# A feed-forward pair's transposes moved between the next pair's second and third quarter

## The chip, the cores and the metric

The kernel runs on one core of one Trainium2 chip. The metric is the device time of one execution in microseconds; three runs of the kernel before gave 3746.26 us as their median (3743.07 to 3754.74). A profile is one further execution recorded by the hardware profiler. The engines are named as the profile names them: PE (TensorE, matmul), PEld (its weight loads), DVE (VectorE), ACT (ScalarE), POOL (GpSimd) and SP (SyncE, which here only issues DMAs).

## The reference

Two layers on x of shape (4, 512, 128, 64): four batch entries, 512 times, 128 frequencies of 64 channels, D = 8192 values at each time, all in float32.

Layer 0, for each batch entry:

```python
xn = layernorm(x)                                  # over D
k, v, r = xn @ Wk, xn @ Wv, sigmoid(xn @ Wr)       # 64 states
s = scan(decay * s + k * v)                        # over time
x = x + (r * s) @ Wo                               # attention
x = x + gelu(conv over the 128 frequencies of layernorm(x))
to = layernorm(depthwise causal conv over time, 3 taps, of layernorm(x))
x = x + to
x = x + (gelu(x @ ffn_W1 + ffn_b1) @ ffn_W2 + ffn_b2)   # 64 -> 256 -> 64
```

Layer 1 takes a moving average over 25 times as the trend, transforms the rest over time with a real FFT, mixes 128 modes with complex weights, transforms back and adds the trend. The change touches only the last line of layer 0, the feed-forward, and how the stages of other batch entries are woven into it.

## The kernel before

In layer 0 the tensors lie with 128 of the D values on the partitions and the 512 times along the free dimension: 64 chunks of 128 x 512 per batch entry, handled in 32 pairs (NPR). The stages of an entry are generator functions: `project` (J, L324), `scan` (Z, L419), `attend_and_convolve` (A, L514), `convolve_time` (C, L645), `open_feed` (O, L705) and `feed_forward` (F, L713). Each `yield` hands over a weight, the share of the stage that has been put out.

`in_turn` (L822) weaves two lines of stages. Its list names for each step which stage of which batch entry runs in the one line and which in the other: F of entry 0 beside J and Z of entry 2, F of 1 beside J and Z of 3, F of 2 beside C and O of 3, and at last F of 3 beside nothing. At every yield it looks which of the two lines is behind and lets that one go on to its next yield. On PE the order so written is the order of execution (`manual_schedule`, L860). On the other engines the framework's scheduler orders the instructions, apart from those that are pinned to the program's order with `keep_in_program_order`. All engines wait for each other through semaphores, and a tile's buffer is reused only once its readers are done.

`run` (L812) keeps a set, `narrowly`. It holds the other stage while that is attention or while its last yield was a step of a chain (a scan, or the broadcast of statistics); it is empty beside the plain steps of `project` and `convolve_time`.

The feed-forward treats a pair in four quarters of the 256 hidden channels:

- `widen(i, q)` (L726; its matmul is L731) multiplies pair i with a quarter of W1: four matmuls of 64 x 64 weights into one of two PSUM units, m and c, which `unit` (L722) gives out alternately. ACT then applies the gelu (L736) and writes `mid`, four buffers.
- `narrow(i, q)` (L738; its matmul is L744) multiplies `mid` with a quarter of W2 and adds it up over the four quarters in two PSUM accumulators, p and pb, each with one buffer. After the fourth quarter DVE adds bias and residual (L757, once for p and once for pb) and writes the pair's result to x4t (three buffers) or, in the last two batch entries, to a wx tile (two buffers).
- `store(i)` (L759) brings the result to time-major form: eight 128 x 128 transposes on PE (L763) into a unit, copies on ACT to `ob` (L771 or L776), and for every second pair a DMA from POOL's queue to x4 (L772). It therefore takes one turn of the same two units that widen uses.

Widen runs two quarters ahead of narrow: in quarters 0 and 1 pair i's own third and fourth widen come, in quarters 2 and 3 the next pair's first two. In quarter 1 the loads and first steps of the residual for pair i + 2 are put out (`residual`, L685: SP's DMAs kx and kh at L605, DVE L690 and L691), in quarter 3 its end (`add_residual`, L694: ACT L699, pinned, and DVE L702).

The loop of the kernel before does this for pair i: first `store(i - lag)`, then the four quarters, then for the first two batch entries one piece of `convolve_ahead` (L633: the first 14 pairs of the next entry's time convolution, in alternate pieces DVE L612 and L615, and ACT L620 with DVE L624), then the yield. Where `narrowly` isn't empty it yields after every quarter. The lag is 1 for entries 0 and 1, and 2 for entries 2 and 3.

So the order on PE around a pair's border, beside a plain stage, is: narrow of the last quarter, the other line's matmuls (L408 for `project`, L251 for `convolve_time`), the transposes, a widen, the next pair's first narrow.

Also touched: `scale_weights` (L354; its instruction L357, DVE) multiplies projection weights by the layernorm's gain. For entries 2 and 3 the call for all steps but the first is pinned. The statistics of these entries (L340) are pinned too.

Of the kernel before, what the change touches and what calls it, by code (L numbers as in the profile page):

```python
# [24 lines left out]
NPR = NCH // 2  # L25
# [54 lines left out]
def layer0(ctx, tc, dram, x, xt, vecs, wkvr, wo, wdec, wconv, fbias, w1, fb1, w2, fb2, x4):  # L80
# [5 lines left out]
    B = x.shape[0]  # L86
# [17 lines left out]
    def two(pool, tag):  # L104
        return pool.tile([P, 2, SL], F32, tag=tag, name=tag)
# [214 lines left out]
    narrowly = set()  # L320
# [3 lines left out]
    def project(b):  # L324
# [36 lines left out]
        ws, xps, xks = {}, {}, {}  # L361
        if b > 1:
            weights(0)
            scale_weights(0, ws[0])
            xps[0] = load_x(b, 0)
        for i in range(NPR):
            first, last = i == 0, i == NPR - 1
# [345 lines left out]
    def feed_forward(b):  # L713
        x3s = opened.pop(b)
        mids, x4s, obs, sums2 = {}, {}, {}, {}
        lag = 1 if b + 2 < B else 2
        turn = [0]
        while not free_s[0]:
            yield BLOCKED
        feeding[0] = True  # L720

        def unit():  # L722
            turn[0] ^= 1
            return two(ps_m, "m") if turn[0] else c_bank()

        def widen(i, q):  # L726
            x3 = x3s[i]
            pm = unit()
            for h in range(2):
                for j in range(2):  # L730
                    nc.tensor.matmul(  # L731
                        pm[halves[j], h, :], lhsT=w1_sb[halves[h], q * H : (q + 1) * H], rhs=x3[halves[h], j, :],
                        start=True, stop=True,
                    )
            mid = mids[i, q] = bk.tile([P, 2, SL], F32, tag="mid", name="mid", bufs=4)
            nc.scalar.activation(mid, pm, AF.Gelu_apprx_tanh, bias=fb1_sb[:, q : q + 1])  # L736

        def narrow(i, q):  # L738
            if q == 0:
                sums2[i] = of_p(), ps_s.tile([P, SL], F32, tag="s", name="pb")  # L740
            mid = mids.pop((i, q))
            for h in range(2):
                for j in range(2):
                    nc.tensor.matmul(  # L744
                        sums2[i][j][halves[h], :], lhsT=w2_sb[halves[j], q, :], rhs=mid[halves[j], h, :],
                        start=q == 0, stop=q == 3,
                    )
            if q < 3:
                return
            x3 = x3s.pop(i)  # L750
            if lag > 1:
                pair = spare("wx", 4 * S + SL)[:, :, 0:SL]
                x4s[i] = [pair[:, j, :] for j in range(2)]
            else:
                x4s[i] = [bk.tile([P, SL], F32, tag="x4t", name="x4t", bufs=3) for _ in range(2)]
            for j, pa in enumerate(sums2.pop(i)):
                nc.vector.scalar_tensor_tensor(x4s[i][j], pa, fb2_sb, x3[:, j, :], ALU.add, ALU.add)  # L757

        def store(i):  # L759
            pt = unit()  # L760
            for j, x4t in enumerate(x4s.pop(i)):
                for t in range(NT):
                    nc.tensor.transpose(pt[:, j, t * P : (t + 1) * P], x4t[:, t * P : (t + 1) * P], ident)  # L763
            s = i // 2
            if i % 2 == 0:
                obs[s] = bk.tile([P, NT, SL], F32, tag="ob", name="ob")
            o = obs[s][:, :, i % 2 * 2 * P : (i % 2 + 1) * 2 * P].rearrange("p t (j w) -> p j t w", j=2)
            pt = pt.rearrange("p j (t w) -> p j t w", t=NT)
            if i % 2:
                for h in range(2):  # L770
                    nc.scalar.copy(o[:, :, :, halves[1 - h]], pt[:, :, :, halves[h]])  # L771
                nc.gpsimd.dma_start(  # L772
                    x4[b][:, s * SL : (s + 1) * SL].rearrange("(t p) d -> p t d", p=P), obs.pop(s)
                )
            else:
                nc.scalar.copy(o, pt)  # L776

        early = None
        done = 0.0
        quarter = 2.25 * (NPR + 1) / (NPR + lag)  # L780
        widen(0, 0)
        widen(0, 1)
        for i in range(NPR + lag):
            if i >= lag:
                store(i - lag)
            for q in range(4):
                done += quarter
                if i < NPR:
                    if q < 2:
                        widen(i, q + 2)  # L790
                    elif i + 1 < NPR:
                        widen(i + 1, q - 2)
                    if i + 2 < NPR and q == 1:
                        coming = residual(b, i + 2)
                    if i + 2 < NPR and q == 3:
                        x3s[i + 2] = add_residual(b, i + 2, *coming)
                    narrow(i, q)
                if q == 3 and b + 2 < B and i > 1:
                    early = early or convolve_ahead(b + 1, lambda: unit()[:, 0, :])
                    next(early, None)  # L800
                if q == 3 or narrowly:
                    yield done
                    done = 0.0
        feeding[0] = False


# [380 lines left out]
```

## Time and profile before

| | |
|---|---|
| median of three runs | 3746.26 us |
| the profiled execution | 3747.14 us |
| its span | 3745.2 us |
| mean granted PE clock | 0.974 |
| PE busy | 3536.6 us, 94% |
| DVE busy | 2669.1 us, 71% |
| ACT busy | 1759.4 us, 47% |
| POOL busy | 522.6 us, 14% |
| HBM traffic | 243 GB/s over the span |

The feed-forwards take these stretches of the span: entry 0 from about 831 to 1235 us, entry 1 from 1490 to 1890, entry 2 from 2145 to 2503, entry 3 from 2503 to 2757; layer 1 takes the last 988 us.

How to read the lines below. In a group, the columns are the line of the kernel, engine, operation, output and inputs with their sizes and the count; then busy time and the mean of one instruction in ns; then the engine's idle time just before these instructions, and what ended most of it. In the timeline, a line has start, duration, engine, line, operation, and in brackets the idle time before it and what ended it. In the table by stretch, a line has its window, length, each engine's busy time, the granted PE clock as a share of full speed, the busy share of the DMA engines and GB/s. A float32 matmul of the program shows as two instructions in the trace.

### The profile page before, as it was taken

The numbers are of one execution on the slowest core, as the hardware profiler recorded it, in microseconds if no ns is written. First come the engines' busy times: TensorE is split into PE (matmuls) and PEld (weight loads), VectorE is DVE, ScalarE is ACT, GpSimd is POOL, SyncE is SP. The second block draws the span as 40 slices with busy tenths as digits, with TensorE's granted clock in tenths as the row PEclk, the third lists the DMA queues.
The fourth block names the chain that finished last, engine by engine and source line by source line (L and its number), as shares of the span: only waits on it lengthen the run. The fifth ranks groups of instructions, "written<-read, shape, count | busy, mean of one in ns | idle before, by whom it ended". The sixth has DMA issues, their size and how long they took to land. (4 is left out here: it accounts for less than half of the span.)

```text
span 3745.2 us, 53017 instructions
## 1 busy us (share of the span) xinstructions
PE 3536.6 (94%) x20041; PEld 1368.8 (37%) x20041; DVE 2669.1 (71%) x3498; ACT 1759.4 (47%) x2299; POOL 522.6 (14%) x782
## 2 busy tenths in 40 slices
PE   9999999999998999999999989999988999989998
PEld 4433322234333223433322233333323843328533
DVE  4445569976776896677789799946667277892677
ACT  0013346655656565565656578868854200142100
POOL 0000012310101121001112122100013000130000
PEclk9999999999999999999999999999999999999999
DMA  9867648787875688788568678645567478993687
GB/s 316 276 206 245 226 163 269 255 280 267 288 263 169 233 279 273 267 292 281 178 231 285 214 248 267 232 152 192 201 233 262 156 235 294 316 322 127 214 285 265
DMA packets 429269, 913.42 MB, mean 244 GB/s; under 512 B 33240, under 2 KB 83672, under 8 KB 424920
## 3 DMA queue, kind: packets, MB, share of 16 engines
q1 hardware_dynamic: 351088, 636.91, 52.4%
q0 software_dynamic: 75776, 271.62, 20.0%
q8 instruction: 160, 2.62, 0.3%
q10 hardware_dynamic: 2152, 1.51, 0.1%
q14 instruction: 93, 0.76, 0.1%
HBM read 641.40 MB, written 268.50 MB: 243 GB/s over the span
## 5 line engine op out<-in xcount | busy, mean ns | idle before, releaser
L744 PE MATMUL p<-mid,w_sb 64*64 64x512 f32 x2048 | 554.8, 599 | 20.2 <-DVE wx L757 20.2
L744 PE MATMUL pb<-mid,w_sb 64*64 64x512 f32 x2048 | 536.7, 599 | 0.0
L736 ACT ACTIVATE mid<-c,fb_sb 128x1024 f32<-128x1024 f32 x256 | 284.6, 1112 | 97.5 <-PE c L731 95.1
L736 ACT ACTIVATE mid<-m,fb_sb 128x1024 f32<-128x1024 f32 x256 | 284.9, 1113 | 93.6 <-PE m L731 92.2
L731 PE MATMUL c<-x,w_sb 64*64 64x512 f32 x2016 | 280.7, 610 | 13.2 <-ACT mid L736 6.9
L731 PE MATMUL m<-x,w_sb 64*64 64x512 f32 x2016 | 283.2, 613 | 6.7 <-ACT ob L776 4.9
L744 PEld LDWEIGHTS p<-mid,w_sb 64*64 64x64 f32 x2048 | 155.5, 135 | 294.8 <-issue 261.6
L408 PE MATMUL a<-xp,wx 128*128 128x512 f32 x512 | 241.7, 615 | 9.1 <-DVE wx L357 8.6
L1032 ACT COPY two<-a 128x512 f32<-128x512 f32 x64 | 37.5, 586 | 428.3 <-PE a L1027 428.3
L1055 PE MATMUL b<-xin,avg_sb 128*128 128x512 f32 x512 | 230.8, 593 | 3.3 <-DVE xin L1061 3.3
L1061 DVE TENSOR_TENSOR xin<-b,pm 128x512 f32<-128x512 f32 x256 | 159.1, 684 | 98.0 <-PE b L1058 83.1
L569 ACT ACTIVATE sq<-x 128x1024 f32<-128x1024 f32 x128 | 135.1, 1055 | 179.4 <-DVE x L566 179.2
L624 DVE SCALAR_TENSOR_TENSOR to<-kd,vec,to 128x510 f32<-128x510 f32 (+1 forms) x272 | 197.2, 745 | 9.9 <-ACT to L620 8.7
L924 DVE COPY xf<-b 128x256 f32<-128x256 f32 x128 | 54.4, 425 | 199.1 <-PE b L1001 179.9
L699 ACT ACTIVATE kd<-kd,vec 128x512 f32<-128x512 f32 x256 | 192.8, 803 | 3.2 <-DVE kd L691 3.2
L251 PE MATMUL st<-x,ones 128*32 128x512 f32 x512 | 173.0, 609 | 12.8 <-DVE x L566 12.8
L624 DVE SCALAR_TENSOR_TENSOR z<-x,vec,z 128x511 f32<-128x511 f32 x240 | 175.9, 745 | 5.3 <-ACT z L620 3.0
L702 DVE TENSOR_TENSOR x<-kd,kx 128x1024 f32<-128x1024 f32 x126 | 154.1, 1223 | 32.6 <-ACT kd L699 32.5
L530 DVE TENSOR_TENSOR x<-a,xp 128x1024 f32<-128x1024 f32 x128 | 156.1, 1220 | 29.1 <-PE a L528 26.9
L528 PE MATMUL a<-rst,wo_sb 64*128 64x512 f32 x512 | 149.2, 657 | 25.1 <-DVE x L530 23.3
L567 POOL DMA_DIRECT2D x<-x x128 | 93.6, 731 | 560.4 <-DVE x L566 544.7
L757 DVE SCALAR_TENSOR_TENSOR x4t<-p,fb_sb,x 128x512 f32<-128x512 f32 x64 | 47.9, 748 | 170.6 <-PE pb L744 168.1
(267 smaller groups left out, 6859.6 us busy)
## 6 DMA issues: line engine op xcount, KB each, us to landing
xp<-in_xt SPq DMA_DIRECT2D x256, 512.0 KB
xin<-x SPq DMA_DIRECT2D x128, 1024.0 KB
kh<-to SPq DMA_DIRECT2D x156, 512.0 KB
x<-x POOLq DMA_DIRECT2D x128, 512.0 KB, 4.6
kx<-x SPq DMA_DIRECT2D x128, 512.0 KB
x<-ob POOLq DMA_DIRECT2D x64, 1024.0 KB, 7.9
out<-xin POOLq DMA_DIRECT2D x64, 1024.0 KB, 6.3
x<-x SPq DMA_DIRECT2D x96, 512.0 KB
```

Source lines behind the costliest of these rows:

```text
L251: nc.tensor.matmul(st[32 * q : 32 * q + 32, :], lhsT=ones, rhs=src[:, j, :], start=first, stop=last,)
L408: nc.tensor.matmul(pa[:, k, :], lhsT=wq[:, j, k * P : (k + 1) * P], rhs=xp[:, j, :], start=first and j == 0, stop=last and j == 1,)
L528: nc.tensor.matmul(at[:, j, :], lhsT=wo_sb[js, :], rhs=rst[js, :], start=True, stop=True)
L530: nc.vector.tensor_tensor(x1, at, xp, ALU.add)
L624: tap = nc.vector.scalar_tensor_tensor(to[:, j, k:], xr[:, j, : SL - k], vec[:, w, c], to[:, j, k:], ALU.mult, ALU.add)
L699: tc.keep_in_program_order(nc.scalar.activation(d[:, j, :], d[:, j, :], AF.Identity, bias=vec[:, B4, c], scale=vec[:, G4, c]))
L702: nc.vector.tensor_tensor(x3, d, x2, ALU.add)
L731: nc.tensor.matmul(pm[halves[j], h, :], lhsT=w1_sb[halves[h], q * H : (q + 1) * H], rhs=x3[halves[h], j, :], start=True, stop=True,)
L736: nc.scalar.activation(mid, pm, AF.Gelu_apprx_tanh, bias=fb1_sb[:, q : q + 1])
L744: nc.tensor.matmul(sums2[i][j][halves[h], :], lhsT=w2_sb[halves[j], q, :], rhs=mid[halves[j], h, :], start=q == 0, stop=q == 3,)
L1055: nc.tensor.matmul(po[j], lhsT=avg_sb[:, j, :], rhs=xin[:, j, :], start=True, stop=False)
L1061: nc.vector.tensor_tensor(by_n(xin[:, j, :]), by_n(po[j]), by_c(pm[j % 2][:, j // 2, :]), ALU.add)
```

## The change

The transposes of pair i - lag no longer stand ahead of pair i's first quarter but between its second and third. The regular yield, at which the other line is let in, stands there too, just ahead of the transposes, and not at the pair's end. Where `narrowly` isn't empty, there is still a yield ahead of each of the other quarters. The lag of the last batch entry becomes 1 (its results stay in wx tiles); that of entry 2 stays 2. The pairs past the end, which only store, yield first. The first scaling of projection weights for entries 2 and 3 is pinned in program order like the others.

```diff
-            scale_weights(0, ws[0])
+            scale_weights(0, ws[0], True)
...
-        lag = 1 if b + 2 < B else 2
+        lag = 2 if b == B - 2 else 1
...
-            if lag > 1:
+            if b + 2 >= B:
                 pair = spare("wx", 4 * S + SL)[:, :, 0:SL]
...
         for i in range(NPR + lag):
-            if i >= lag:
-                store(i - lag)
-            for q in range(4):
-                done += quarter
-                if i < NPR:
+            if i < NPR:
+                for q in range(4):
+                    if q == 2:
+                        if done:
+                            yield done
+                        done = 0.0
+                        if i >= lag:
+                            store(i - lag)
+                    elif done and narrowly:
+                        yield done
+                        done = 0.0
                     if q < 2:
                         widen(i, q + 2)
                     elif i + 1 < NPR:
...
                     narrow(i, q)
-                if q == 3 and b + 2 < B and i > 1:
-                    early = early or convolve_ahead(b + 1, lambda: unit()[:, 0, :])
-                    next(early, None)
-                if q == 3 or narrowly:
-                    yield done
-                    done = 0.0
+                    done += quarter
+            else:
+                yield done
+                done = 4 * quarter
+                store(i - lag)
+            if b + 2 < B and i > 1:
+                early = early or convolve_ahead(b + 1, lambda: unit()[:, 0, :])
+                next(early, None)
+        yield done
         feeding[0] = False
```

## The prediction

> **What bounds the kernel.** I read the page's busy shares first, then the busy times by stretch, then the groups of instructions around the feed-forward, then the timeline of single pairs.
>
> ```profile
> PE 3536.6 (94%) x20041; PEld 1368.8 (37%) x20041; DVE 2669.1 (71%) x3498; ACT 1759.4 (47%) x2299; POOL 522.6 (14%) x782
> ```
>
> ```profile
> 831.00:1141.00 310.00, 302.95 (x2056) 122.26 (x2052) 221.65 (x299) 188.24 (x213) 27.13 (x32) 0.99 0.80 272
> 2177.00:2463.00 286.00, 264.89 (x2207) 97.03 (x2200) 263.39 (x296) 246.85 (x291) 52.15 (x70) 0.98 0.74 245
> 2504.00:2750.00 246.00, 246.00 (x2172) 97.03 (x2168) 149.09 (x148) 201.06 (x226) 10.56 (x14) 1.00 0.52 174
> ```
>
> PE is busy 94% of the span. The three stretches (length, then busy time of PE, its weight loads, DVE, ACT and POOL, granted clock, DMA share) are the feed-forward of batch entry 0 beside the projection of entry 2, that of entry 2 beside the time convolution of 3, and that of 3 alone; entry 1 beside projection 3 reads as entry 0 does (302.67 of 310). In the first and last PE has no gap worth naming, so what makes PE wait there lengthens the kernel. In the stretch of entry 2, DVE (263.39 of 286) and ACT (246.85) are nearly as full as PE.
>
> Inside a pair, the four quarters are alternately widen (L731) and narrow (L744), each 0.86 us of PE at full rate (two steps of 0.43 us in the timeline): 4 x 1.72 = 6.9 us. The eight transposes (L763) are 1.04 us, with the switches of tile shape about 1.25; a step of projection (L408) is 3.7.
>
> After the fourth narrow, DVE empties the two accumulators with L757, one after the other. Each accumulator has one buffer, so the next pair's first narrow waits for both:
>
> ```profile
> L744 PE MATMUL p<-mid,w_sb 64*64 64x512 f32 x2048 | 554.8, 599 | 20.2 <-DVE wx L757 20.2
> L757 DVE SCALAR_TENSOR_TENSOR x4t<-p,fb_sb,x 128x512 f32<-128x512 f32 x64 | 47.9, 748 | 170.6 <-PE pb L744 168.1 <-PE p L744 2.5
> L757 DVE SCALAR_TENSOR_TENSOR x4t<-pb,fb_sb,x 128x512 f32<-128x512 f32 x64 | 47.5, 742 | 0.1
> ```
>
> and in the timeline of a pair of entry 0:
>
> ```profile
> 930.87 0.59 PE L744 MATMUL p<-mid,w_sb 64*64 64x512 f32 x2
> 931.41 3.70 PE L408 MATMUL a<-xp,wx 128*128 128x512 f32 x8
> 934.95 1.04 PE L763 MATMUL m<-ident,x4t 128*128 128x128 f32 x8
> 935.91 1.09 PE L731 MATMUL c<-x,w_sb 64*64 64x512 f32 x8
> ```
>
> Here is the cover as it stands: after the narrow at 930.87, PE does 3.7 us of projection, the transposes and one widen before it needs the accumulators again at 936.8. DVE frees them by 932.9. The wait is paid by nobody.
>
> One pair of the same trace has no cover. With lag 2, the second pair of entry 3 has no transposes yet, and nothing stands beside it:
>
> ```profile
> 2503.70 0.60 PE L744 MATMUL p<-mid,w_sb 64*64 64x512 f32 x2
> ...
> 2504.13 1.04 PE L731 MATMUL m<-z,w_sb 64*64 64x512 f32 x8
> ...
> 2504.37 0.75 DVE L757 SCALAR_TENSOR_TENSOR wx<-p,fb_sb,z 128x512 f32<-128x512 f32 x1 [10.21 <-PE pb L744]
> ...
> 2505.03 0.74 DVE L757 SCALAR_TENSOR_TENSOR wx<-pb,fb_sb,z 128x512 f32<-128x512 f32 x1
> 2505.17 0.19 PEld L744 LDWEIGHTS p<-mid,w_sb 64*64 64x64 f32 x2 [0.88 <-DVE wx L757]
> ...
> 2505.83 0.13 PEld L744 LDWEIGHTS pb<-mid,w_sb 64*64 64x64 f32 x1 [0.47 <-DVE wx L757]
> ```
>
> Only the widen (2504.13, over at 2504.99) stands between two narrows; the second accumulator is released at 2505.83. From this pair's last narrow to the next pair's is 2503.70 to 2511.47, 7.77 us, where 6.86 us is matmul: **0.91 us lost**. This is exactly the order that the change gives to nearly every pair.
>
> **The skill.** "PSUM — Partial Sum Buffer" (section on PSUM bank collisions) says the queues of ScalarE and VectorE are strict FIFO and matmuls start in program order; the trace agrees: nothing behind the waiting L744 runs until 2505.83. "TensorE: Matmul & The Clock Gate" (Part 1) says the clock drops to half after an idle window of about 3.4 us. The trace agrees in size: the stretch 2233 to 2241, after a gap of 2.4 us and a half-covered one of 0.7, has a granted clock of 0.79.
>
> **The change, part by part.** The sums are against the profiled run, 3747.1 us (span 3745.2); the median of the three runs, 3746.3, is within 1 us of it.
>
> *Entries 0 and 1.* Each has 26 pairs beside the projection, 307.6 us or 11.83 per pair: 11.53 in one, 12.07 in the next, where PE waits 0.54 us for ACT. After the change, the projection and transposes stand between the second and third quarter. Between narrow 4 and the next narrow 1 is one widen, so each pair gets +0.91. In the new order of ACT, the two L620 of the convolution made ahead and the ob copy fall under the projection's 3.7 us, and L699 under another quarter, so the 0.54 may vanish, 0.27 per pair. That gives +0.64 to +0.91; I take 0.75: 52 x 0.75 = **+39**.
>
> *Where a scan or attention is let in*, the line is still called at each quarter, ahead of the first too, so cover remains: 0. The transposes no longer wait for L757 there (15.1 + 9.1 us of PE idle before L763), but narrow then waits instead; I count -8 to +8.
>
> *Entry 3, alone.* Lag 2 to 1. Before, the transposes of an older pair and the widen, 2.1 us, cover the wait almost exactly; a pair takes 8.15 us. After, only the widen covers: +0.91 x 30 = **+27**. One lagged pair less at the end, one fresh wait of 1.5 us there: 0.
>
> *Entry 2.* Here the order on three engines closes a loop:
>
> ```profile
> 2309.95 1.05 ACT L771 COPY ob<-c 128x512 f32<-128x512 f32 x2
> 2310.90 0.83 ACT L620 ACTIVATE z<-x,vec 128x512 f32<-128x512 f32 x1
> ...
> 2313.52 1.53 DVE L624 SCALAR_TENSOR_TENSOR z<-x,vec,z 128x511 f32<-128x511 f32 x2
> 2315.09 1.23 DVE L612 TENSOR_TENSOR x<-xp,rm 128x1024 f32<-128x1024 f32 x1
> 2316.35 1.23 DVE L615 TENSOR_TENSOR x<-x,rm 128x1024 f32<-128x1024 f32 x1
> 2317.49 0.74 DVE L757 SCALAR_TENSOR_TENSOR wx<-p,fb_sb,x 128x512 f32<-128x512 f32 x1
> ```
>
> The second L620 is behind the ob copy on ACT, and L624, L612, L615 are ahead of L757 on DVE, before and after alike. What moves is PE: the ob copy needs the transposes, and they now come after narrow 1, which needs L757. From the release at 0: narrow, widen, narrow 2.7; L251 0.96 and switch 3.8; transposes 4.9; ob 5.9 (two copies, 1.05); L620 6.7; two L624 8.2; L612 and L615 10.6; two L757 **12.0 us**. Done the same way for the order of before, the ob copy comes at 3.5 to 4.5 behind L699, L620 and L671, the widen waits for it, and 9.8 results, which the trace shows (2296.25, 2306.01, 2315.85). So +2.2 for a pair with one convolution step. In the order of after there are 12 of these, +26. Five times two steps fall together; those two pairs take 11.5 + 13.75 now, and 14.9 + 12.3 by the same addition, +2 each, +10. Five pairs at the end have none: 5 x 0.9. Sum **+41**.
>
> *Clock.* The loop leaves PE idle about 2 us and then half idle 0.7 per pair. A half-rate window of 3.4 us costs 1.7. Bounds 0 and 22 x 1.7 = 37; I take a third, **+12**, since a somewhat longer gap did drop it.
>
> *The pinned L357* (6 x 0.31 us) stands near its matmul instead of some 370 us ahead; DVE is idle there, 0. If its weights come late, one wait of the size seen once (4.3 us). *DMAs:* the pair's kx and kh loads on SP and the ob store on POOL keep their order against each other and move by half a pair past the projection's loads. At a DMA share of 0.80 and longer pairs they should stay hidden: 0, at worst 2 us per late step. *Buffers* of x4t and wx are freed half a pair later than before and needed at the next fourth quarter, two quarters (3.4 us) later: 0.
>
> Sum: 39 + 27 + 41 + 12 = +119, from 3746: **3865 us**.
>
> **Rivals.** *A: the bare wait alone.* The loop of entry 2 isn't as tight (L612 and L615 run earlier, or pairs with two steps had hidden slack): 39 + 27 + 0 to 25 gives +66 to +91, about 3825. For it: the 0.91 is seen, the loop is added up. Against: the same addition gives 9.8.
> *B: faster.* The waits that go (24 us before L763 for L757, 11 us before L731 for the ob copies) are the whole effect: 3746 - 35 = 3711. It decides if both L757 end within the widen's 0.86 us; they take 1.45 us or more after the narrow's end in every pair, so it would need a second accumulator buffer.
> *C: worse.* Half clock in every pair of entry 2, L757 late behind waiting projection weights on DVE: +170 and more, 3920.
> *D: no effect*, if the other line's matmuls still came before the first narrow. The order of after shows them behind the second, except in the scan.
>
> **Numbers.** A change of 0.3% (11 us) is about what a measurement of this kernel can tell from none. My forecast 0.57, A 0.23, C 0.12, B 0.05, D 0.03. Faster 0.05, same 0.03, slower 0.92. The range 3800 to 3930 takes A's low end nearly whole and most of C.
>
> **What would show it.** L744 p and pb, idle for DVE L757 in nearly every pair, about 100 us in sum, where 20 stood; in the stretch of entry 3 a pair of 9.05 us; beside the projection 12.4; in entry 2 singles of 12 with L757 starting 2 us after narrow 4 ended. If entry 2 stays at 9.8 to 10.7, A is right; if L744 shows no wait, I am wrong altogether.

## The result and the profile after

The changed kernel takes 3981.2 us (median, 3976.6 to 3986.9) where the kernel before took 3743.1 in the same session: a ratio of 1.063, 95% interval 1.061 to 1.065. It is slower, as forecast, by about twice the forecast: 238 us where 119 were expected, and outside the range. The profiled execution has a span of 3980.1 us and a mean granted clock of 0.954; the span before was 3745.2.

The busy shares of the changed kernel:

```profile
PE 3683.2 (93%) x20041; PEld 1435.7 (36%) x20041; DVE 2679.8 (67%) x3498; ACT 1761.5 (44%) x2299; POOL 520.6 (13%) x782
```

The number of instructions is the same on every engine, and DVE, ACT and POOL are busy for as long as before, to within 0.5%. PE, with the same matmuls, is "busy" for 147 us more: part of a wait is booked as a longer matmul, and matmuls at half clock are longer too. The table by stretch (window, length, busy time of PE, its weight loads, DVE, ACT and POOL, granted clock, DMA share, GB/s) for the feed-forwards of entries 0 to 3:

```profile
848.50:1143.00 294.50, 264.09 (x1644) 110.42 (x1636) 172.67 (x233) 149.56 (x170) 22.00 (x26) 0.95 0.68 230
1559.00:1856.00 297.00, 264.95 (x1648) 110.79 (x1640) 173.50 (x237) 150.27 (x170) 21.86 (x26) 0.95 0.68 231
2289.00:2622.00 333.00, 268.82 (x1808) 92.37 (x1804) 245.72 (x268) 207.56 (x246) 45.04 (x63) 0.85 0.55 183
2715.00:2990.00 275.00, 275.00 (x2220) 112.86 (x2216) 149.05 (x148) 207.55 (x229) 11.30 (x15) 1.00 0.46 159
```

Beside the projection PE was busy 98% of the time; now it is 90%. In entry 2 the clock went from 0.98 to 0.85. Entry 3 shows PE busy all the time, although each pair has a wait in it. The groups of narrow (L744), busy time, mean in ns, then PE's idle time before them:

```profile
L744 PE MATMUL p<-mid,w_sb 64*64 64x512 f32 x2048 | 738.3, 638 | 142.0 <-DVE wx L757 77.0 <-DVE x4t L757 64.6
L744 PE MATMUL pb<-mid,w_sb 64*64 64x512 f32 x2048 | 572.9, 637 | 1.4 <-DVE wx L757 1.4
```

The wait ahead of narrow is 142 us where it was 20.2, nearly all of it for L757 (x4t in entries 0 and 1, wx in entries 2 and 3). To see where the time went, I measure each feed-forward from the end of its first pair's L757 to the end of its last pair's, in us:

| | entry 0 | entry 1 | entry 2 | entry 3 | ahead of and between them, layer 1 |
|---|---|---|---|---|---|
| before | 401.5 | 389.4 | 340.7 | 250.4 | |
| after | 439.3 | 440.8 | 441.7 | 275.2 | |
| difference | +37.8 | +51.4 | +101.0 | +24.8 | +19.9 |

Of the last column, 14.5 us lie ahead of entry 0. That start varies from 834 to 850 us over the runs below (837 in another run that holds the whole change), most of it already at the first matmul of the projection of entry 2. Part of it may be the pinned scaling (see its run below); the cause stays open.

A plain pair beside the projection takes 12.4 us and a pair of entry 3 8.93, as forecast (12.4 and 9.05). But in each of entries 0 and 1 there are also ten pairs in a row of 14 to 21 us, and in entry 2 a single pair takes 14.0 us, not 12.0. The timeline of a long pair in entry 0 (start, duration, engine, line; in brackets the idle time before and what ended it):

```profile
972.97 1.28 DVE L340 BATCH_NORM_STATS2 stt<-sq 128x6 f32<-128x512 f32 x2
974.27 0.37 SPq L332 DMA_DIRECT2D sq<-in_x  x1
974.74 0.46 SPq L350 DMA_DIRECT2D wx<-in_wkvr  x1
...
984.19 0.55 DVE L357 TENSOR_SCALAR wx<-wx,vec 128x192 f32<-128x192 f32 x2 [9.95 <-DMA wx<-in_wkvr]
984.66 0.74 DVE L757 SCALAR_TENSOR_TENSOR x4t<-p,fb_sb,x 128x512 f32<-128x512 f32 x1
985.32 0.74 DVE L757 SCALAR_TENSOR_TENSOR x4t<-pb,fb_sb,x 128x512 f32<-128x512 f32 x1
985.45 0.29 PEld L744 LDWEIGHTS p<-mid,w_sb 64*64 64x64 f32 x2 [8.30 <-DVE x4t L757]
985.46 1.11 PE L744 MATMUL p<-mid,w_sb 64*64 64x512 f32 x1 [7.42 <-DVE x4t L757]
```

The projection weights are asked for at 974.74 and land 9.4 us later. DVE stands in front of their scaling all that time, and L757, whose accumulators are long complete, stands behind it. The load goes out no sooner because on SP it is behind a load of x (L332), whose buffer comes free only when the statistics L340 end on DVE, and on DVE the scaling is the next instruction after these statistics. In the pairs of 12.4 us the load goes out a pair ahead (for one at 948.27, its scaling at 961.70) and nothing waits. Every second of the ten long pairs has such a wait, of 8.8 to 11.2 us in entry 0. And a single pair of entry 2:

```profile
2500.46 1.23 DVE L612 TENSOR_TENSOR x<-xp,rm 128x1024 f32<-128x1024 f32 x1
2501.72 1.22 DVE L615 TENSOR_TENSOR x<-x,rm 128x1024 f32<-128x1024 f32 x1
2502.87 0.74 DVE L757 SCALAR_TENSOR_TENSOR wx<-p,fb_sb,x 128x512 f32<-128x512 f32 x1
...
2503.66 0.28 PEld L744 LDWEIGHTS p<-mid,w_sb 64*64 64x64 f32 x2 [3.55 <-DVE wx L757]
2503.66 1.11 PE L744 MATMUL p<-mid,w_sb 64*64 64x512 f32 x1 [2.67 <-DVE wx L757]
...
2505.42 2.02 PE L731 MATMUL m<-x,w_sb 64*64 64x512 f32 x8
...
2509.35 0.82 ACT L620 ACTIVATE z<-x,vec 128x512 f32<-128x512 f32 x1 [0.67 <-PE a L251]
...
2511.01 1.05 ACT L771 COPY ob<-c 128x512 f32<-128x512 f32 x2
...
2511.95 0.82 ACT L620 ACTIVATE z<-x,vec 128x512 f32<-128x512 f32 x1
...
2516.78 0.74 DVE L757 SCALAR_TENSOR_TENSOR wx<-p,fb_sb,x 128x512 f32<-128x512 f32 x1
```

L757 is behind two normalisations, as forecast. After the wait of 2.67 us the widen takes 2.02 us instead of 1.04: half clock. ACT's first L620 waits 0.67 us for L251, a wait that my addition didn't have. The second L620 stands behind the ob copy, as it did in my addition.

### The profile page after: what moved, and what is told of

It is laid out like the page before. It is cut to its first block, busy times and chain, and to the rows that moved or that the text cites. A ratio compares the mean times of both kernels' runs of the same rounds, so it can differ in the third digit from the quotient of the medians.

```text
span 3980.1 us, 52944 instructions
## 1 busy us (share of the span) xinstructions
PE 3683.2 (93%) x20041; PEld 1435.7 (36%) x20041; DVE 2679.8 (67%) x3498; ACT 1761.5 (44%) x2299; POOL 520.6 (13%) x782
## 5 line engine op out<-in xcount | busy, mean ns | idle before, releaser
L744 PE MATMUL p<-mid,w_sb 64*64 64x512 f32 x2048 | 738.3, 638 | 142.0 <-DVE wx L757 77.0
L744 PE MATMUL pb<-mid,w_sb 64*64 64x512 f32 x2048 | 572.9, 637 | 1.4 <-DVE wx L757 1.4
L744 PEld LDWEIGHTS p<-mid,w_sb 64*64 64x64 f32 x2048 | 198.9, 142 | 413.4 <-issue 154.9
L731 PE MATMUL c<-x,w_sb 64*64 64x512 f32 x2016 | 327.8, 639 | 0.4 <-ACT mid L736 0.4
L731 PE MATMUL m<-x,w_sb 64*64 64x512 f32 x2016 | 320.5, 622 | 2.7 <-ACT ob L776 1.8
L624 DVE SCALAR_TENSOR_TENSOR z<-x,vec,z 128x511 f32<-128x511 f32 x240 | 176.8, 747 | 88.7 <-ACT z L620 83.9
L624 DVE SCALAR_TENSOR_TENSOR to<-kd,vec,to 128x510 f32<-128x510 f32 (+1 forms) x272 | 197.6, 747 | 10.4 <-ACT to L620 9.3
L744 PEld LDWEIGHTS pb<-mid,w_sb 64*64 64x64 f32 x2048 | 142.9, 142 | 118.4 <-issue 50.5
L251 PE MATMUL st<-x,ones 128*32 128x512 f32 x512 | 171.6, 613 | 13.1 <-DVE x L566 13.0
```

What stands on the lines that cost most here:

```text
L251: nc.tensor.matmul(st[32 * q : 32 * q + 32, :], lhsT=ones, rhs=src[:, j, :], start=first, stop=last,)
L624: tap = nc.vector.scalar_tensor_tensor(to[:, j, k:], xr[:, j, : SL - k], vec[:, w, c], to[:, j, k:], ALU.mult, ALU.add)
L731: nc.tensor.matmul(pm[halves[j], h, :], lhsT=w1_sb[halves[h], q * H : (q + 1) * H], rhs=x3[halves[h], j, :], start=True, stop=True,)
L744: nc.tensor.matmul(sums2[i][j][halves[h], :], lhsT=w2_sb[halves[j], q, :], rhs=mid[halves[j], h, :], start=q == 0, stop=q == 3,)
```

## The experiments

Ratios are against the kernel before in the same session. "Entry" lengths are measured as above.

### Weights behind the eviction

The changed kernel, with DVE's L340 and L357 of the projection ordered behind the last L757 put out before them:

```diff
-                nc.vector.scalar_tensor_tensor(x4s[i][j], pa, ...)
+                last757[0] = nc.vector.scalar_tensor_tensor(x4s[i][j], pa, ...)
...
-                    tc.keep_in_program_order(scaled)
+                    tc.keep_in_program_order(scaled); behind_eviction(scaled)
...
-                    tc.keep_in_program_order(stats)
+                    tc.keep_in_program_order(stats); behind_eviction(stats)
```

> Edit to the changed kernel: on DVE the projection's statistics (L340) and weight scalings (L357) stand behind the evictions L757 of the pair before, not ahead. My theory now: where entries 0 and 1 stand beside the projection, the pairs that cost 20 to 24 us instead of 12.4 do so because L757 queues on DVE behind an L357 that waits for its weights' DMA. Then all those pairs take 12.4, L757 starts 0.05 us after narrow's end, entries 0 and 1 together lose 55 to 70 us, entry 2 and 3 stay (14.0 and 8.93 a pair), total about 3915. Rival: the projection needs these weights itself, so the wait only moves to L408; the total stays within 10 us of 3981.

Measured: 3898.3 us, ratio 1.041 (1.039 to 1.043), 83 us less than the change. Entries 0 and 1 take 405.1 and 403.7 us (34 and 37 less); 9.6 us of the rest is the early start. All ten long pairs are gone in both entries, every plain pair takes 12.4 us:

```profile
974.06 0.54 DVE L357 TENSOR_SCALAR wx<-wx,vec 128x192 f32<-128x192 f32 x2
980.17 0.75 DVE L757 SCALAR_TENSOR_TENSOR x4t<-p,fb_sb,x 128x512 f32<-128x512 f32 x1 [1.98 <-PE pb L744]
980.84 0.74 DVE L757 SCALAR_TENSOR_TENSOR x4t<-pb,fb_sb,x 128x512 f32<-128x512 f32 x1
980.98 0.19 PEld L744 LDWEIGHTS p<-mid,w_sb 64*64 64x64 f32 x2 [0.88 <-DVE x4t L757]
```

L757 now waits for PE and not the other way round, and what is left is the bare wait of 0.88 us that the prediction saw in the kernel before. So about 71 us of the loss is this queue. Entries 0 and 1 are now 18 us longer than before (808.8 against 790.9). That is less than the 39 of the forecast because these entries had long pairs of their own before, which are gone here: 20.3 us in entry 0 and 19.5 in entry 1, and at the end of entry 0 18.3 and 18.6, some 26 us above their neighbours. The last two are gone in the changed kernel already (12.9 and 13.2); the run of the pinned scaling below shows why.

### The transposes alone

The transposes between the second and the third quarter, but the other line let in at the pair's border, as before. The lag of 1 in entry 3 and the pinned scaling of the change stay in:

```diff
-                    if q == 2:
-                        if done:
-                            yield done
-                        done = 0.0
-                        if i >= lag:
-                            store(i - lag)
-                    elif done and narrowly:
+                    if done and (q == 0 or narrowly):
                         yield done
                         done = 0.0
+                    if q == 2 and i >= lag:
+                        store(i - lag)
```

> One part of the change alone: the transposes stand between second and third quarter, but the other line is let in at the pair's border as before. My theory (what costs is that the other line's matmuls no longer cover the evictions): beside the projection 11.5 to 11.8 us a pair, no wait of L744; entry 2, where both L620 now stand ahead of the ob copy, near 10; entry 3 stays at 8.93, since there the transposes were the cover. Total 3760 to 3785. Rival (the place of the transposes itself costs, through the units m and c): pairs beside the projection over 12 and a total above 3850.

Measured: 3803.7 us, ratio 1.016 (1.014 to 1.018), above what I expected. Entry 2 takes 343.0 us with single pairs of 10.0: in entry 2 the transposes' place costs next to nothing. Entry 3 loses the 24.8 us of the whole change, since its lag of 1 stays and nothing is let in there. Beside the projection pairs take 11.8 and 12.75 us in turn, not 11.5 to 11.8; entries 0 and 1 take 403.1 and 402.5. There the widen behind the transposes waits for a gelu that now stands behind two L620 on ACT:

```profile
926.52 1.52 ACT L620 ACTIVATE z<-x,vec 128x512 f32<-128x512 f32 x2 [0.59 <-DVE x L615]
927.19 1.09 PE L763 MATMUL m<-ident,x4t 128*128 128x128 f32 x8
927.94 1.09 ACT L736 ACTIVATE mid<-c,fb_sb 128x1024 f32<-128x1024 f32 x1
...
929.09 1.09 PE L731 MATMUL c<-x,w_sb 64*64 64x512 f32 x8 [0.81 <-ACT mid L736]
```

### Two accumulators in entry 3

The changed kernel, where the odd pairs of entry 3 add up in the two banks of tile a, which nothing else uses by then:

```diff
+                if b == B - 1 and i % 2:
+                    pair2 = two(ps_a, "a")
+                    sums2[i] = pair2[:, 0, :], pair2[:, 1, :]
+                else:
+                    sums2[i] = of_p(), ps_s.tile([P, SL], F32, tag="s", name="pb")
```

> Edit to the changed kernel: in entry 3 alone every odd pair uses the two banks of tile a, idle there, as its accumulators, every even one p and pb. My theory (the single buffer of p and pb is the wait): the pair falls from 8.93 to 8.0 or 8.15, entry 3 loses 25 to 30 us, the rest stays, total about 3953. Rival (the wait is DVE's or the units', which this doesn't touch): 8.93 stays.

Measured: 3950.7 us, ratio 1.055 (1.053 to 1.057), 30 us less than the change, with pairs of 8.05 us and an entry 3 of 247.9. The single buffer of the accumulators is what makes the wait of entry 3.

### DVE's order in entry 2 as well

The first experiment, and entry 2's L612 ordered behind L757 too:

```diff
-        first = nc.vector.tensor_tensor(xr, x2, pair_of(rb), ALU.mult)
+        first = nc.vector.tensor_tensor(xr, x2, pair_of(rb), ALU.mult); behind_eviction(first if b == B - 1 else None)
```

> The edit of e1 and, for the time convolution of entry 3, the same: its first DVE operation L612 stands behind the L757 of the pair before. My theory: entry 2's loop (L757, narrow, transposes, ob copy, second L620, L624, L612, L615, L757) is one of order; both L620 now stand ahead of the ob copy, a pair with one convolution step falls from 14.0 to 9.9 to 10.4, the half-clock windows of entry 2 go, total 3840 to 3860. Rival (DVE and ACT are simply full there): 12 or more a pair stays, total above 3890.

Measured: 3882.7 us, ratio 1.037 (1.035 to 1.039). L757 starts 0.05 us after the narrow's end in most pairs, as meant, but single pairs still take 11 to 14 us and entry 2 takes 417.7, 24 less than in the change: my expectation fails, and so does the rival's total. The wait has moved to the next queue:

```profile
2313.53 1.22 DVE L615 TENSOR_TENSOR x<-x,rm 128x1024 f32<-128x1024 f32 x1
...
2314.79 1.52 ACT L620 ACTIVATE z<-x,vec 128x512 f32<-128x512 f32 x2 [2.69 <-DVE x L615]
...
2316.21 0.99 ACT L776 COPY ob<-m 128x1024 f32<-128x1024 f32 x1
2317.25 0.30 PEld L731 LDWEIGHTS m<-x,w_sb 64*64 64x64 f32 x8 [3.54 <-ACT ob L776]
2317.25 1.99 PE L731 MATMUL m<-x,w_sb 64*64 64x512 f32 x8 [2.66 <-ACT ob L776]
```

L612 and L615 now come later, L620 waits for them on ACT, the ob copy stands behind L620, and the widen waits for the unit that the ob copy reads. It is a wait as long as the one of 2.67 us before narrow, at another place.

### The pinned scaling alone

```diff
-            scale_weights(0, ws[0])
+            scale_weights(0, ws[0], True)
```

> The kernel before with one edit of the change alone: the first scaling of the projection's weights (L357) is held to program order. My forecast priced this at 0. The three variants run so far that keep it all start the feed-forward of entry 0 some 5 to 15 us later than the kernel before does, with the first late step in the stage ahead of it. If the pinned scaling is the cause: that start goes from about 836 us to 841-850 and the total to 3752-3762 us, with pairs of 11.4 and 12.2 us beside the projection as before. If it is not: within 3 us of before, and the delay comes from the new order elsewhere.

Measured, on the kernel before: 3745.9 us, ratio 1.0006 (0.9992 to 1.0020). The total doesn't move, so the expected 3752 to 3762 us fails. Within the profile two things do move. Entry 0 takes 390.6 us instead of 401.5, since its two long pairs of 18.3 and 18.6 us are now 12.8 and 13.5. In the kernel before, the first scalings of entry 3's weights, not pinned to a place, stand in these pairs, wait for their loads, and L757 stands behind them:

```profile
1161.43 0.55 DVE L357 TENSOR_SCALAR wx<-wx,vec 128x192 f32<-128x192 f32 x2 [4.33 <-DMA wx<-in_wkvr]
1161.90 0.74 DVE L757 SCALAR_TENSOR_TENSOR x4t<-p,fb_sb,x 128x512 f32<-128x512 f32 x1
```

So the queue that costs most in the change can be seen in the kernel before. The first of these two pairs takes 17.2 us or more in all eight profiles without the pin and 14.4 or less in all nine with it. And entry 0 starts at 842.9 us, 7 later, as expected of a pin that is the cause; over all profiles it starts at 837 to 850 us with the pin (mean 845) and at 834 to 846 without (mean 839). The ranges overlap, so this isn't settled.

### Letting in alone

The kernel before, where only the yield moves between the second and the third quarter:

```diff
             for q in range(4):
+                if done and (q == 2 or narrowly):
+                    yield done
+                    done = 0.0
                 done += quarter
...
-                if q == 3 or narrowly:
-                    yield done
-                    done = 0.0
+        yield done
         feeding[0] = False
```

> The kernel before with the place of letting in alone changed: the other line comes between the second and the third quarter, while the transposes stay ahead of the first quarter with their old lags, and the first scaling is not pinned. My theory by now: the weights of the projection still arrive in front of L757 on DVE, so about 35 us per entry in entries 0 and 1, +70; no bare wait, since the transposes still stand between; entry 3 unchanged at 8.15 us a pair; entry 2 needs both moves for its loop, so its single pairs are 10 to 10.7 us and it lasts 340 to 365 us. Together 3815 to 3845 us. The rival, that the parts only add up (the whole change +235, the transposes alone +59), gives 3746 + 176 = 3922 us, with entry 2 at about 440.

Measured: 3935.4 us, ratio 1.051 (1.049 to 1.053), near the rival's total, and my theory of that moment is wrong on two points. First, entries 0 and 1 take 460.0 and 447.5 us, longer than in the whole change: the transposes, ahead of the first narrow, read what L757 writes, so they wait for it themselves, and a plain pair takes 13.0 us (11.5 + 1.5) besides the late weights. Moving the transposes away is what brings this to 12.4. Second, entry 2 doesn't need both moves: single pairs take 13.5 us, and the entry 406.3 (the rival's 440 fails there).

```profile
2423.64 1.23 DVE L612 TENSOR_TENSOR x<-xp,rm 128x1024 f32<-128x1024 f32 x1
...
2424.90 1.23 DVE L615 TENSOR_TENSOR x<-x,rm 128x1024 f32<-128x1024 f32 x1
...
2426.04 0.74 DVE L757 SCALAR_TENSOR_TENSOR wx<-p,fb_sb,x 128x512 f32<-128x512 f32 x1
...
2426.84 1.17 PE L744 MATMUL p<-mid,w_sb 64*64 64x512 f32 x2 [1.64 <-DVE wx L757]
...
2433.04 0.82 ACT L620 ACTIVATE z<-x,vec 128x512 f32<-128x512 f32 x1 [0.76 <-PE a L251]
...
2433.95 3.14 DVE L624 SCALAR_TENSOR_TENSOR z<-x,vec,z 128x511 f32<-128x511 f32 x4 [2.85 <-ACT z L620]
...
2437.12 1.23 DVE L612 TENSOR_TENSOR x<-xp,rm 128x1024 f32<-128x1024 f32 x1
```

The ring can be read from this: L757 frees narrow, the let-in L251 comes after narrow, L620 waits for L251, L624 for L620, and L612, L615 and the next L757 stand behind L624 on DVE. No transpose and no ob copy is in it. This is read from the trace; no run shows that opening this ring alone shortens the pair. The total met the sum of parts by chance: by entry, the parts (+58.5, +58.1, +65.6, +0.1 here; +1.6, +13.1, +2.3, +24.8 for the transposes) don't add up to the whole in entries 0 to 2.

The clock falls here as well. Two stretches that follow each other in this pair (columns as in the table above, the granted clock third from the end):

```profile
2424.27:2427.69 3.42, 1.78 (x13) 0.43 (x13) 3.38 (x5) 3.08 (x4) 0.59 (x1) 1.00 0.65 171
2427.69:2431.10 3.41, 3.41 (x20) 1.69 (x16) 3.33 (x3) 0.00 (x0) 0.00 (x0) 0.50 0.71 238
```

PE was idle for 1.64 us before this, and its weight loads for 2.52.

### The stall filled with matmuls

The changed kernel with work that adds nothing to the output, ahead of the first narrow in entry 2:

```diff
+                    if q == 0 and still[0] is not None:
+                        for _ in range(4):
+                            nc.tensor.matmul(still[0], lhsT=ident, rhs=x3s[i][:, 0, :], start=True, stop=True)
                     narrow(i, q)
```

> The changed kernel with four more matmuls of 128x512 in each pair of entry 2, put just ahead of the pair's first narrow, into a bank that nothing reads (1.75 us of work that adds nothing to the output). PE stands still there for some 2.7 us. If about 1.2 us of a 14.0 us pair is lost because the clock is halved after that stall, keeping PE busy brings the clock of the stretch from 0.85 to 0.95 or more and single pairs to 12.6-13.0 us; entry 2 lasts 410-420 us where it was 442, and the total falls by 20 to 30 us to 3950-3960 us. If the pair is long by its chain of waits alone, the clock may rise but single pairs stay at 13.8-14.3 us and the total at 3975 us or above; the last pairs, whose wait is only 0.9 us, then lose about 1 us each.

Measured: 3969.4 us, ratio 1.060 (1.058 to 1.062). The stretch with the convolution, of this kernel:

```profile
2290.00:2560.00 270.00, 265.43 (x1780) 91.22 (x1772) 221.76 (x240) 185.37 (x220) 40.08 (x56) 1.00 0.63 208
```

The clock is 1.00 there and single pairs take 12.9 us instead of 14.0, with more work in them. The total fell less than expected because the four matmuls take 3.70 us and not the 1.75 that I had put down; so the last pairs, which have almost no stall, lose 2.9 us each. Over the 23 pair periods with convolution the gain is 348.5 - 318.1 = 30.4 us, over the last eight the loss is 12.5. At least 30 us of entry 2's 101 are thus half clock; the added matmuls may hold back a part. The added matmuls end within 0.4 us of the second L757, so a chain at full clock without them could hardly be much shorter than 12.6 us.

### Weights behind the eviction, in the kernel before

The order of the first experiment in the kernel before, without the change:

```diff
+                    tc.keep_in_program_order(scaled); behind_eviction(scaled)
...
+                    tc.keep_in_program_order(stats); behind_eviction(stats)
```

> The kernel before, with the statistics and the scaling of the projection's weights (L340, L357) ordered behind the last L757 on DVE, as in the first experiment. In the kernel before, two pairs at the end of entry 0 have L757 behind such a scaling (18.3 and 18.6 us), and one more waits for weights in front of the projection's matmul (20.3 us). If that order is what costs there: these two fall to 14-15 us, 6 to 12 us in all, 3735 to 3741 us. If the scaling comes late for its own matmul instead: plain pairs longer by 0.1 us or more and no gain, 3745 to 3755 us.

Measured: 3737.1 us, ratio 0.999 (0.997 to 1.000). Of the two long pairs at the end of entry 0 one went from 18.6 to 13.6 us, the other stayed at 17.5; the pin alone had taken both away. A gain of 0.1% is less than this measurement can tell from none.

### More room for the convolution, in place

Three kernels with one line of entry 2's convolution changed, in letting-in alone, in the whole change, and in the previous kernel:

```diff
-                    x2, xr, to, sq = spare("xp", SL), spare("x1", SL), spare("z", SL), two(bk, "sq")
+                    x2 = xr = spare("xp", SL); to, sq = spare(("z", "x1")[k % 2], SL), two(bk, "sq")
```

> The previous let-in-alone kernel, with one line of entry 2's convolution changed: L612 and L615 work in place in the loaded tile, and the convolution's result goes by turns to z and to the tile so freed, seven buffers in place of four. In that kernel the first L620 of a step waits about 0.7 us for L251, which stands behind the pair's first narrow, which waits for L757, which is queued behind the L612 and L615 that L620 and L624 hold up. If this return through the buffers of z closes the loop, single pairs go from 13.5 to 10.0-10.9 us, entry 2 from 406 to 335-365 us, the total from 3935 to 3875-3895 us. If the loop is closed by the orders of ACT and DVE alone, single pairs stay at 13.0-13.6 us and the total within 8 us of 3935.

> The same line changed in the whole change. If the buffers of z close the loop here too, what is left is the ob copy that stands between two L620 on ACT and needs the transposes behind the first narrow, the loop that I added up in the forecast at 12.0 us: single pairs fall from 14.0 to 11-12.5 us with the clock of the stretch above 0.9, entry 2 from 442 to 380-415 us, the total from 3981 to 3920-3955 us. If the wait of L620 for L251 is a mere 0.65 us in a chain that other things close, single pairs take 13.2-14.0 us and the total is 3965-3981 us.

> The kernel before, with weights behind L757 as in the experiment before and the same line changed in entry 2. PE waits some 27 us there for L757 and the ob copies. If z's buffers hold part of the convolution back there too, entry 2 falls from 341 to 330-337 us and the total to 3725-3735 us. If not, 3735 to 3745 us, with single pairs of 9.9 to 10.1 us as they are.

Measured, in this order: 3923.9 us (ratio 1.048) with entry 2 at 386.6, a miss for the theory's numbers and for the rival's; 3938.8 us (ratio 1.052) with entry 2 at 403.4 and singles of 11.9, inside them; and 3831.1 us (ratio 1.023) with entry 2 at 432.3, 91 us longer than without the line. The waits of DVE in the third kernel's entry 2 (who waited for whom: sum, times, longest) say why:

```profile
DVE xp L612 <- DMA xp<-x: 78.9, 20, 6.1
```

The loaded tile is now held until L624 is done, so the next load is issued later, and L612 waits for it. The line costs by itself what it was meant to measure, and can't price the buffers, in the second kernel either, where the numbers came as expected.

### A fifth buffer for z

So the same question with nothing else moved: every fifth step writes to the memory of x4t, which is idle then.

```diff
+                    to = bk.tile([P, 2, SL], F32, tag="x4t", name="z", bufs=1) if k % 5 == 4 else spare("z", SL)
+                    x2, xr, sq = spare("xp", SL), spare("x1", SL), two(bk, "sq")
...
-                x4s[i] = [bk.tile([P, SL], F32, tag="x4t", name="x4t", bufs=3) for _ in range(2)]
+                pair = bk.tile([P, 2, SL], F32, tag="x4t", name="x4t", bufs=1)
+                x4s[i] = [pair[:, j, :] for j in range(2)]
```

> The whole change, with a fifth buffer for z: every fifth step of entry 2's convolution writes to the memory of x4t, which nothing uses then (x4t becomes one tile for both halves, which is enough with a lag of 1). If the return L757, narrow, L251, z, L620, L624, L612, L615, L757 sets the pair, L620 no longer waits for L251 and single pairs fall from 14.0 to 11-12.5 us (what is left is the ob copy between two L620), entry 2 from 442 to 380-415 us, the total to 3920-3955 us. If z's wait is 0.65 us in a chain that is closed otherwise: 13.3 us or more, entry 2 at 425 or more, the total at 3965 or more.

> Letting-in alone, with the fifth buffer for z. If the return through z sets the pair there: from 13.5 to 9.9-11 us, entry 2 from 406 to 340-365 us, the total from 3935 to 3870-3900 us. If the queue orders of DVE and ACT close it without z: 12.8 us or more, entry 2 at 390 or more, the total at 3915 or more.

> The kernel before with weights behind L757 and the fifth buffer for z. In it L251 stands ahead of the pair's first narrow, so z comes free in time; I expect single pairs of 9.8 to 10.1 us, as they are, and 3730 to 3745 us in all. If more buffers let the convolution run ahead of the feed-forward: singles of 9.2 to 9.7 us, entry 2 at 325-335 us and 3722-3732 us. More than 3750 us would say that the edit itself costs something, as the in-place version did.

Measured, in this order: 3973.3 us (1.062), entry 2 at 442.1; 3940.8 us (1.053), entry 2 at 410.4, singles 13.5; 3740.6 us (0.9997, 0.9985 to 1.0009). The edit costs nothing and brings nothing. In the timeline of letting-in alone with it, L620 still waits for L251:

```profile
2450.43 0.82 ACT L620 ACTIVATE z<-x,vec 128x512 f32<-128x512 f32 x1 [1.52 <-PE a L251]
```

Counted off in the traces, L620 was three steps ahead of L251 with four buffers and is four steps ahead with five. The convolution runs as far ahead as its buffers let it, and then again waits for the newest L251. The number of buffers doesn't set the pair; I had read the wait as its cause.

### DVE's order in letting-in alone

The order of the fourth experiment (its L340 and L357 too), in the kernel with letting-in alone:

```diff
+        first = nc.vector.tensor_tensor(xr, x2, pair_of(rb), ALU.mult); behind_eviction(first if b == B - 1 else None)
...
+                if done and (q == 2 or narrowly):
+                    yield done
```

> Letting-in alone, with L340, L357 and entry 2's L612 ordered behind the last L757 on DVE. If the loop is L757, narrow, L251, L620, L624, L612, L615, L757, it opens here: L757 starts at most 0.7 us after the fourth narrow in entry 2 where it starts 3.0 us after it, single pairs go from 13.5 to 10.0-11.3 us, entry 2 from 406 to 345-370 us; in entries 0 and 1 the pairs of 16 to 20 us go to 13.0 to 15 us, since the transposes still wait for L757 of the pair just ended. The total falls from 3935 to 3800-3835 us. If another chain closes it (the first L620 behind L251 on ACT with the ob copy behind it), single pairs stay above 12 us as they did in the whole change with this order, and the total above 3840 us.

Measured: 3869.0 us, ratio 1.033 (1.030 to 1.036). The long pairs of entries 0 and 1 are gone (417.9 and 415.8 us), as expected. Entry 2 is even longer, 421.5 us, with singles of 12.2 to 13.6: the rival's numbers came. L757 starts some 0.2 us after narrow's end, so this arc of the ring is open, and the wait is elsewhere, though not where the rival put it:

```profile
2420.20 0.71 POOL L630 TENSOR_TENSOR z<-z,vec 128x4 f32<-128x4 f32 x1 [6.11 <-DVE z L624]
2420.76 0.74 DVE L757 SCALAR_TENSOR_TENSOR wx<-p,fb_sb,x 128x512 f32<-128x512 f32 x1
2420.96 1.06 ACT L671 ACTIVATE sq<-z 128x1024 f32<-128x1024 f32 x1 [1.68 <-POOL z L630]
...
2421.93 1.10 ACT L736 ACTIVATE mid<-m,fb_sb 128x1024 f32<-128x1024 f32 x1
2422.92 1.11 ACT L736 ACTIVATE mid<-c,fb_sb 128x1024 f32<-128x1024 f32 x1
2423.08 1.09 PE L763 MATMUL m<-ident,wx 128*128 128x128 f32 x8 [2.51 <-ACT mid L736]
```

Two gelus, which PE needs, are behind the square L671, which waits for POOL, which waits for L624. What stays open is an order of all three queues under which letting in behind the narrow would cost nothing in entry 2; none was found.

## Why the prediction was wrong

Its direction and its first mechanism hold: the cover goes from between the last narrow and the next first one, and the bare wait is 0.88 us. Its parts, one by one:

- **Entries 0 and 1, +39.** The plain pair of 12.4 us is right to 0.05 (the sum took +0.75 a pair, which would make it 12.6). The two entries lost 89 us, and 71 of it came back when the weights were ordered behind L757.
- **The pinned L357 and the DMAs, each 0.** The pin is worth nothing in the total, as said, but not because DVE was idle: it takes some 11 us from entry 0, which the +37.8 of entry 0 has in it. What failed is the step that the loads "should stay hidden: 0, at worst 2 us per late step". In the long pairs of entry 0 the weights' load takes 8.3 to 10.7 us from issue to landing. SP issues it only when the statistics ahead of the scaling are done on DVE, and the scaling's place on DVE is ahead of L757, so the whole load is waited for. I had the rule in the text, that what is queued behind a waiting instruction waits too (on the skill's page "PSUM — Partial Sum Buffer" it stands in the section "Engine vs sequencer instructions"), and applied it to PE only. Rival C names this very queue, at 0.12; it came on top of the forecast case and not in place of it.
- **The let-in stages, 0 (-8 to +8).** No run tells them apart. In entry 1 the last seven pair periods, where the scan is let in, take 95.8 us after and 94.9 before.
- **Entry 3, +27.** Measured +24.8; the pair is 8.93 us for a forecast of 9.05. Two accumulators take it back.
- **Entry 2, +41, and the clock, +12.** Measured +101. Every member of the forecast's loop stands in the changed kernel's trace in the forecast's order, but a round takes 13.9 us (narrow from 2503.66 to 2517.58) and not 12.0. From narrow to L251 are 4.6 us where 2.7 stood, mostly because of the half clock, +1.9; the ob copy starts 0.7 us after the transposes end, behind the first L620 and L671 on ACT, which that sum left out; and the next narrow starts after the first L757, -0.7. What failed in the mechanism is what it was put down to: that the ob copy needs the transposes behind the narrow. With the transposes alone moved the pair stayed at 10.0 us, while letting in alone, with no ob copy between, made 13.5 of it. Without the clock entry 2 loses at most about 70 us where 41 stood.
- **The clock** is that part's mis-sized term: 30 us or more, not 12. The bounds of 0 and 37 held the 30. The skill's page "TensorE: Matmul & The Clock Gate", in the section "HAM oscillation — how this bites in real kernels", describes a kernel that goes back to half clock in every tile because each has one wait; that is what this trace shows. The idle window of about 3.4 us of the page's Part 1, by which the prediction went, isn't needed here: the clock halved at a PE wait of 2.67 us in the changed kernel and of 1.64 us in letting-in alone. The weight loads stood still for 3.55 and 2.52 us in these waits (PEld L744), so they give no limit of 3.4 us either.
- **What was not forecast** beyond that is the 20 us ahead of and between the entries, mostly the start of entry 0, without a cause found.

Against rivals A, B and D the result is plain: the wait is there, it is paid, and it isn't all. What came is rival C, both its half clock and its queue. The range ended at 3930 because I took the queue and the clock as one unlikely case. The sum as the runs give it, of the two profiled spans: 18 us net for the bare wait in entries 0 and 1, 71 for the weights there, 25 for entry 3, about 70 for the order of the queues and 30 for the clock in entry 2, 20 without a cause; 234 of the 235 us. The split of entry 2 rests on one run, and which wait sets its pair stays open: two runs that took the wait at L757 away found others in its place.

Nothing that was tried beats the kernel before by more than can be measured: 3737.1 us with the weights behind L757 is the best, at a ratio of 0.999.

## What to carry to other kernels

When a step is moved on one engine, go through the other engines' queues for instructions that wait for what the step triggers, above all for a DMA: here 10 us of load latency stood in front of an eviction that was ready. When a stage has PE, DVE and ACT all nearly full, opening one wait in a fixed order of three queues moves it to the next queue (L757, then the ob copy, then the gelu); price the ring as a whole. A wait that recurs in every pair should be priced with the half clock that may follow it: here 1.64 us of idle PE in a pair of 13.5 us was enough. And the kernel before is worth reading for the new wait: here two pairs had it already.

## What was not expected of the hardware

- More work took less time: 3.70 us of matmuls that nothing reads brought the granted clock of a stretch from 0.85 to 1.00 and a pair from 14.0 to 12.9 us. A stall of 2.67 us in a pair of 14 us was enough to lose the full clock again in nearly every pair, and so was one of 1.64 us in a pair of 13.5 (letting-in alone).
- PE's busy time is no measure of its waits: the stretch of entry 3 shows 275.00 of 275.00 us busy in the changed kernel, while every pair has the wait of 0.9 us, which shows as a matmul of 1.07 us instead of 0.59 and as idle time of the weight loads. The skill says as much in "Perfetto Trace Analysis", section "Identifying the Most-Contended Engine", that matmul busy time is a bad measure; this trace agrees.
